# A sixteen-stage network in one kernel: an earlier search in the second attention, and joint exponentials ahead of the two state space models

## The chip, the cores and the metric

The kernel runs on one core of a Trainium2 chip. The metric is device time in microseconds (us), the time from the program's start to its end on that core. A core has five engines that run side by side, each with its own instruction stream: TensorE (PE, matrix products; its weight loads are listed as PEld), VectorE (DVE), ScalarE (ACT, functions such as exp by table), GpSimd (POOL) and SyncE (SP), which here issues DMA transfers. A stream is worked off in order, so an instruction that waits holds everything behind it on its engine. Matrix products are written to PSUM, a memory of a few banks of 128 x 512 numbers each, and the other engines read them from there.

## What is computed

A tensor x of 4 batches, 512 tokens and 128 channels (fp32) passes 16 stages of the form x = x + f(layernorm(x)): four rounds of attention a, feed-forward, attention b, feed-forward. They are called L0a L0f L0b L0f, L1a L1f L1b L1f, L2a L2f L2b L2f, L3a L3f L3b L3f. The change touches three places. The first is L0b, an attention of 16 heads of 8 dimensions that keeps the most important keys:

```python
scores = jnp.einsum('bhqd,bhkd->bhqk', q, k) * inv_sqrt_d
scores = jnp.where(causal[None, None], scores, -jnp.inf)
attn_weights = jax.nn.softmax(scores, axis=-1)
mean_importance = attn_weights.mean(axis=2)
mean_importance = mean_importance.at[:, :, -RECENCY:].set(1.0)    # RECENCY = 64
_, idx = jax.lax.top_k(mean_importance, k_keep)                    # k_keep = 391 of 512
K_keep = jnp.take_along_axis(k, idx_e, axis=2)                     # V_keep likewise
a2 = jax.nn.softmax(jnp.einsum('bhqd,bhkd->bhqk', q, K_keep) * inv_sqrt_d, axis=-1)
out = jnp.einsum('bhqk,bhkd->bhqd', a2, V_keep)
```

The other two are the state space models L2b and L3b, of which only the first steps matter here; they stand behind L2f (a mixture of 8 experts, two of which are kept for a token, beside a shared one) and L3f (a gated recurrence over the four batches):

```python
u = silu(conv(x @ in_proj_x) + conv_b)                  # 256 channels; z = x @ in_proj_z
dtr, Bc, Cc = split(u @ x_proj)                         # 64, 16, 16
delta = softplus(dtr @ dt_proj + dt_proj_b)
h = exp(delta * A) * h + (delta * u) * Bc               # scan over the 512 tokens
y = (sum_n h * Cc + u * D) * silu(z)                    # then y @ out_proj
```

## The kernel before, in words

The stages are methods of one class and run one after the other; the order of a stage's instructions is written out by hand. `keep` pins an instruction's place in the order of its engine, and `Plan` is a list of steps, each with the number of the loop step at which it is issued. Line 346 is the helper that records every matmul, so matmuls are told apart by the tile that they write.

**L0b (from line 745).** Heads are held as 4 groups g of 4 heads i; q and k have 32 rows per head, of which 8 hold the head and row 8 a one (in q) and the mask (in k); row 9 of q takes the negated largest score. Its first part is a loop over n = 0 to 67. Step n < 64 is one (batch, group, block of 128 queries): `weights(n)` does the scores of four heads (`ps_s`), adds the causal mask and finds the minimum of the negated scores in one DVE instruction per head (line 839), and takes the exponential with its sum on ACT (line 850). `invert(n - 2)` takes reciprocals (line 861), and `importance(n - 4)` adds the weighted columns up in one PSUM bank `imp` per half (two batches, 32 steps). `choose(half)` is a generator for the search: its first call copies the negated importance into `neg` (line 890) and stops; each of the next 16 does one MAX8 (line 897) and, when called again, MATCH_REPLACE8 (line 899), so 121 keys or a few more in whole eights are struck out; then it makes the mask (line 903) and issues eight DMAs on SP (line 908) that put it into row 8 of each head of k. In the loop one `next(choice)` is issued at each step with n % 7 < 4 from n = 36 on.

In the second part, unit n = 0 to 63 is one (batch, group, block of 128). `largest(n, i)` makes a head's scores of 128 queries against all 512 keys again, now with the mask, and takes the maximum on DVE (line 925). After four units `into_q` transposes these into row 9 of q: four transposes on PE and one addition on DVE (line 983). `weigh(n, i)` then makes the transposed scores `ps_st` and their exponential on ACT (line 1007), `gather` multiplies with the values, `divide`, `turn` and `project` finish. The units 0, 1, 2 of `largest` stand at n = 64, 65, 66 of the first loop. The rest is the list `stream`, in which `weigh(n)` alternates with `largest(n + 5)`; it begins with the units 3 and 4 of `largest`, and after each last head of a unit the second search (`choose(1)`) does one step. All these banks come from one ring of 7.

**L2f (line 1897).** For each batch the loop of `experts` (line 615) does 13 `hidden` steps (line 1923): two products `ps_1` and `ps_3`, ACT's Identity with bias into `t` (line 1931), DVE's product (line 1932), ACT's Silu into `hc` (line 1935); then the weighted sums `ps_o`. So m runs over 52 hidden steps, and the first steps of L2b are laid among them by the list `self.extra`: pairs of a step number m and a piece of `mamba_ahead`. Both kinds of products come from rings of four banks per tag.

**mamba_ahead (line 1973).** It prepares batch 0 of a state space model: `norm`, `turn` (transposes), `conv`, `xd`, `br`, `cr` (projections), `gate`, and the softplus, written as max(y, 0) + ln(1 + exp(-|y|)) with a correction of the rounding, for the two halves c of the 256 channels: `step(c)` (line 2069) makes `ps_dt`, DVE takes max(y, 0) into dl, ACT does Abs and Exp (2075, 2076); `log(c)` does Ln on ACT (2081) and two DVE operations (2082, 2084); `rest(c)` does three elementwise operations, on DVE for c = 0 and on POOL for c = 1 (2095), and stores dl to DRAM by a DMA on SP (2096). `spare` is true in L2f and false in L3f.

**L3f (2765 to 2791) and mamba (2143).** The end of L3f runs the pieces of `mamba_ahead` and the layer norms of batches 1 to 3 (`self.centred`, line 393: four DVE instructions of 128 x 128 each); what it leaves is in `self.late`, pairs of a scan step and a piece. The loop of `mamba` has 64 scan steps (16 per batch): a step n fetches the rates of step n + 5 from DRAM (SP, line 2268), multiplies (DVE, line 2293), scans twice (DVE, line 2298), multiplies by cr (POOL, line 2301), makes `ps_du` of step n + 1 on PE and the exponential (decay, ACT, line 2282) of step n + 3, then a piece of `prepare` for the next batch, every other step `read` (PE), and at its end the pieces of the plan.

Of the kernel before, what the change touches and what calls it, by code (L numbers as in the profile page):

```python
# [12 lines left out]
AF = mybir.ActivationFunctionType  # L13
ALU = mybir.AluOpType
# [260 lines left out]
class Net:  # L275
# [469 lines left out]
    def L0b(self):  # L745
# [7 lines left out]
        with ExitStack() as es:  # L753
# [176 lines left out]
            def split(n):  # L930
                return n // 16, n // 4 % 4, n % 4


            later = {}
            project_q(0, 0, bank("ps_qk"))
# [7 lines left out]
                    later[4 * g + h + 18] = f, 3, g  # L943
            choice = iter(())
            LATE = 4
            AHEAD = 3
            for n in range(64 + LATE):
                if n < 64:
                    weights(n)
                if n == 2:  # L950
                    rest()
                    clear(vt[0])
                if 2 <= n <= 65:
                    invert(n - 2)
                if 64 <= n < 64 + AHEAD:
                    for i in range(4):
                        largest(n - 64, i)
                if n >= LATE:
                    importance(n - LATE)
                if n == 31 + LATE:  # L960
                    choice = choose(0)
                if n in later:
                    f, b, g = later[n]
                    f(b, g, bank("ps_qk"))
                if n < 36 or n % 7 < 4:
                    next(choice, None)
            for _ in choice:
                pass
            choice = choose(1)

            def into_q(n):

                b, g, _ = split(n)
                nm = nmt[n // 4 % 2]
                pt = bank("ps_t", (P, CB, P))
                for j in range(CB):
                    self.tr(pt[:, j], nm[:, j].rearrange("p i r -> p (i r)"))  # L980
                qb = q[g][:, b * S : b * S + S]
                keep(
                    nc.vector.tensor_tensor(qb, qb, pt.rearrange("p j t -> p (j t)"), ALU.add)  # L983
                )

            def values(b):
                pv = bank("ps_v", (P, CB, 16, 8))
# [69 lines left out]
                    )  # L1057
                self.add_to_x(b, px)

            LAG = 5  # L1060
            stream = [(largest, n, i) for n in range(AHEAD, LAG) for i in range(4)]
            plan = Plan()
            for a in range(64):
                if a % 16 == 0:
# [13 lines left out]
                if a % 16 == 15:  # L1078
                    plan.at(m + 13, turn, a // 16)
                    plan.at(m + 18, project, a // 16)  # L1080

            plan.at(4 * (4 - AHEAD) + 4, into_q, 3)
            for m in range(len(stream) + 20):
                plan.run(m)
                if m < len(stream):
                    f, n, i = stream[m]
                    f(n, i)
                    if f is largest and i == 3:
                        next(choice, None)


# [805 lines left out]
    def L2f(self):  # L1897

        nc, tc = self.nc, self.tc
        NH = 13  # L1900
        with (
            tc.tile_pool(name="l2f_s", bufs=1) as sp,
            tc.tile_pool(name="l2f_r", bufs=3) as rp,
            tc.tile_pool(name="l2f_p", bufs=4, space=PSUM) as pp,
            tc.tile_pool(name="l2f_d", bufs=1, space=DRAM) as dp,
        ):
            xT, rest = self.norm(pp)
            w1, w3, w2 = self.W("f2_w1"), self.W("f2_w3"), self.W("f2_w2")
            b1, b3 = self.W("f2_b1"), self.W("f2_b3")

            def gates(b, cw):
                pl = pp.tile([P, CB, 8], F32, tag="u", name="ps_l")
                for j in range(CB):
                    c = b * S + j * P
                    self.mm(pl[:, j], xT[:, c : c + P], self.W("f2_gw"), pin=True)
                pr = self.softmax_tok(rp, pl, 8)
                bi = rp.tile([P, CB, 8], F32, name="bi")
                gb = self.row("f2_gb").unsqueeze(1).to_broadcast([P, CB, 8])
                nc.vector.tensor_tensor(bi, pr, gb, ALU.add)
                t2 = self.top2(rp, bi, pr, 8)  # L1920
                nc.vector.tensor_copy(cw, t2)

            def hidden(b, m, hc):
                n = P if m < NH - 1 else 48
                xb, cs = xT[:, b * S : b * S + S], slice(m * P, m * P + n)
                p1 = pp.tile([P, S], F32, tag="mm", name="ps_1")
                self.mm(p1[:n], w1[:, cs], xb, pin=True)
                p3 = pp.tile([P, S], F32, tag="u", name="ps_3")
                self.mm(p3[:n], w3[:, cs], xb, pin=True)
                t = rp.tile([P, S], F32, name="t")  # L1930
                nc.scalar.activation(t[:n], p1[:n], AF.Identity, bias=b1[:n, m : m + 1])  # L1931
                nc.vector.scalar_tensor_tensor(  # L1932
                    t[:n], p3[:n], b3[:n, m : m + 1], t[:n], ALU.add, ALU.mult
                )
                nc.scalar.activation(hc[:n, m], t[:n], AF.Silu)

            f = self.follow
            if f:

                def bank(name):  # L1940
                    return pp.tile([P, S], F32, tag="u", name=name)

                self.extra = tuple(
                    (at, f[n], *a, bank)
                    for at, n, *a in (
                        (4, "rates"),
                        (5, "constants"),
                        (22, "norm", 0, 1),
                        (23, "turn", 0),
                        (25, "conv", 0),  # L1950
                        (27, "conv", 1),
                        (29, "xd"),
                        (30, "step", 0),
                        (30, "step", 1),
                        (30, "log", 0),
                        (30, "log", 1),
                        (31, "rest", 0),
                        (32, "rest", 1),
                        (34, "br"),
                        (35, "cr"),  # L1960
                        (37, "gate", 0),
                        (38, "gate", 1),
                        (44, "norm", 1, 3),
                        (45, "turn", 1),
                        (46, "turn", 2),
                    )
                )
                self.late = ((0, f["norm"], 3, 4), (2, f["turn"], 3))
            self.experts(
                (sp, rp, pp, dp), NH, 48, 11, 8, 176, gates, hidden, w2, rest, bias=True  # L1970
            )

    def mamba_ahead(self, g, spare):
# [20 lines left out]
        xd = sz[:64, 0]  # L1994
        if spare:

            e0, w0, l0, e1 = (
                self.xn[:, CB * b : CB * b + CB].rearrange("p j d -> p (j d)") for b in range(B)
            )
        else:  # L2000
            m["sets"][1] = self.mamba_set(sp, 1)
            e0, w0, l0, e1 = (m["sets"][1][i][:, c] for i in range(2) for c in range(2))
        e, wl, ln = (e0, e1), (w0, sz[:, 0]), (l0, sz[:, 1])

        def rates(bank):

# [62 lines left out]
        def step(c, bank):  # L2069
# [2 lines left out]
            ps = bank("ps_dt")  # L2072
            self.mm(ps, w["dw"][:, c * P : c * P + P], xd, pin=True)
            keep(nc.vector.tensor_scalar(dl[:, c], ps, db, 0.0, ALU.add, ALU.max))
            keep(nc.scalar.activation(e[c], ps, AF.Abs, bias=db))
            keep(nc.scalar.activation(e[c], e[c], AF.Exp, scale=-1.0))

        def log(c, bank):


            keep(nc.scalar.activation(ln[c], e[c], AF.Ln, bias=ones[:, 0:1]))
            keep(nc.vector.tensor_scalar(wl[c], e[c], 1.0, None, ALU.add))
            keep(
                nc.vector.scalar_tensor_tensor(
                    wl[c], wl[c], 1.0, e[c], ALU.subtract, ALU.subtract
                )
            )

        def rest(c, bank):
            for o, x, y, op in (  # L2090
                (ln[c], ln[c], wl[c], ALU.subtract),
                (dl[:, c], dl[:, c], ln[c], ALU.add),
                (du[:, c], dl[:, c], u[:, c], ALU.mult),
            ):
                keep((nc.gpsimd if c else nc.vector).tensor_tensor(o, x, y, op))
# [14 lines left out]
            "log": log,  # L2110
            "rest": rest,
        }

# [557 lines left out]
    def L3f(self):  # L2671
# [3 lines left out]
        with (  # L2675
# [90 lines left out]
            if f:  # L2766
# [25 lines left out]


# [51 lines left out]
```

## Time and profile before

| | us |
|---|---|
| median of three runs (2464.59 to 2468.78) | 2466.05 |
| the profiled execution | 2471.9 |
| its span | 2470.2 |
| PE busy in it | 2183.7 (88%) |
| DVE busy | 1751.5 (71%) |
| ACT busy | 1307.5 (53%) |
| POOL busy | 608.9 (25%) |
| PE's weight loads, beside its products | 1025.6 (42%) |

The mean granted clock of PE is 0.926 of full speed. The span holds 32,491 instructions and 126.79 MB of DMA. In the span L0b stands at about 490 to 960, the first L2f ends and L2b begins at about 1617, and L3b runs from about 2169 to 2424.

The profile lists busy time by engine, the chain of work that ended last, and groups of instructions by line and tile. "x" before a number is a count; `out<-in` names the tiles written and read; "idle before" is the time in which the engine had nothing to run just ahead of these instructions, and the arrow names what ended it. Time is counted from the start of the span.

### The profile page before, as it was taken

The numbers are of one execution on the slowest core, as the hardware profiler recorded it, in microseconds if no ns is written. First come the engines' busy times: TensorE is split into PE (matmuls) and PEld (weight loads), VectorE is DVE, ScalarE is ACT, GpSimd is POOL, SyncE is SP. The second block draws the span as 40 slices with busy tenths as digits, with TensorE's granted clock in tenths as the row PEclk, the third lists the DMA queues.
The fourth block names the chain that finished last, engine by engine and source line by source line (L and its number), as shares of the span: only waits on it lengthen the run. The fifth ranks groups of instructions, "written<-read, shape, count | busy, mean of one in ns | idle before, by whom it ended". The sixth has DMA issues, their size and how long they took to land.

```text
span 2470.2 us, 32491 instructions
## 1 busy us (share of the span) xinstructions
PE 2183.7 (88%) x11647; PEld 1025.6 (42%) x11647; DVE 1751.5 (71%) x3544; ACT 1307.5 (53%) x2561; POOL 608.9 (25%) x431
## 2 busy tenths in 40 slices
PE   7999999999899998899877789888868998888867
PEld 2343334733233443567434345442214566422213
DVE  6666666689887675656464674579997557589995
ACT  4555554279645555342442464667635445478642
POOL 1100010010000001022152410048761015148761
PEclk9999999999799999999867889999979999989888
DMA  3000002300000000510200033235542420045540
GB/s 141 1 1 1 1 1 68 72 1 1 2 1 2 1 1 1 112 27 7 100 1 1 0 67 75 56 111 162 148 125 56 87 48 2 1 119 153 152 131 17
DMA packets 68304, 126.79 MB, mean 51 GB/s; under 512 B 9264, under 2 KB 13360, under 8 KB 67504
## 3 DMA queue, kind: packets, MB, share of 16 engines
q1 hardware_dynamic: 68144, 124.73, 19.4%
q8 instruction: 92, 1.51, 0.2%
q14 instruction: 68, 0.56, 0.1%
HBM read 118.93 MB, written 5.64 MB: 50 GB/s over the span
## 4 chain that ended last, share of the span: by engine, by line
PE 61%; DVE 26%; ACT 5%; DMA 3%; issue 2%; POOL 1%; SPq 0%; DVEq 0%; POOLq 0%; ACTq 0%
PE ps_o L346 13%; PE ps_s L346 11%; DVE hc L2298 10%; PE ps_st L346 5%; PE ps_c L346 4%; PE ps L346 4%; DVE ps_du L2293 4%; PE ps_g L346 4%; PE ps_u L346 2%; PE ps_v L346 2%; PE ps_x L346 2%; PE ps_qk L346 2%; DVE xn L393 2%; DVE e L839 2%; PE ps_q L346 2%
## 5 line engine op out<-in xcount | busy, mean ns | idle before, releaser
L2301 POOL TENSOR_TENSOR hc<-hc,cr 128x1024 f32<-128x1024 f32 x126 | 296.0, 2362 | 202.3 <-DVE hc L2298 134.7
L2298 DVE TENSOR_TENSOR_SCAN hc<-da,ps_du 128x512 f32<-128x512 f32 x256 | 298.2, 1206 | 15.6 <-ACT da L2282 2.6
L346 PE MATMUL ps_s<-k,q 32*128 32x512 f32 (+3 forms) x1088 | 275.8, 611 | 16.5 <-DVE mx L839 8.6
L346 PE MATMUL ps_du<-du,spread 64*128 64x512 f32 x512 | 167.5, 730 | 100.3 <-DVE hc L2298 97.9
L538 ACT ACTIVATE e<-ps_s,mx 128x512 f32<-128x512 f32 x256 | 172.6, 686 | 139.9 <-DVE mx L533 133.3
L2282 ACT ACTIVATE da<-da,am 128x512 f32<-128x512 f32 x244 | 165.3, 716 | 96.6 <-DMA da<-dram 82.5
L925 DVE TENSOR_REDUCE nm<-ps_s 128x1 f32<-128x512 f32 x256 | 160.4, 683 | 69.6 <-PE ps_s L346 67.8
L346 PE MATMUL ps<-xT,w_L2f 128*128 128x512 f32 (+1 forms) x416 | 197.1, 621 | 4.0 <-DVE t L1932 4.0
L1007 ACT ACTIVATE e<-ps_st 128x512 f32<-128x512 f32 x256 | 135.3, 601 | 104.9 <-PE ps_s L346 92.4
L533 DVE TENSOR_REDUCE mx<-ps_s 128x2 f32<-128x1024 f32 x128 | 150.9, 1219 | 43.8 <-PE ps_s L346 43.6
L346 PE MATMUL ps_st<-q,k 32*128 32x512 f32 x512 | 167.3, 632 | 6.5 <-DVE q L983 5.5
L2293 DVE TENSOR_TENSOR ps_du<-ps_du,br 128x1024 f32<-128x1024 f32 x128 | 154.8, 1210 | 12.4 <-PE ps_du L346 12.4
L850 ACT ACTIVATE e<-e,mx 128x512 f32<-128x512 f32 (+3 forms) x256 | 140.2, 549 | 20.6 <-DVE mx L839 20.0
L346 PEld LDWEIGHTS ps_s<-k,q 32*128 32x128 f32 x1088 | 96.5, 198 | 113.1 <-DVE mx L839 52.7
L346 PEld LDWEIGHTS ps_du<-du,spread 64*128 64x128 f32 x512 | 46.0, 209 | 214.2 <-DVE hc L2298 184.5
L346 PE MATMUL ps_s<-q,k 64*128 64x512 f32 x512 | 129.1, 618 | 2.2 <-ACT e L538 1.7
L346 PE MATMUL ps_c<-e,vz 128*64 128x512 f32 x512 | 123.5, 604 | 0.8 <-POOL vz L549 0.8
L1932 DVE SCALAR_TENSOR_TENSOR t<-ps,w_L2f,t 128x512 f32<-128x512 f32 (+1 forms) x104 | 76.8, 746 | 63.5 <-PE ps L346 44.4
L346 PEld LDWEIGHTS ps<-xT,w_L2f 128*128 128x128 f32 (+1 forms) x416 | 76.6, 193 | 101.4 <-issue 75.2
L839 DVE CUSTOM_DVE_ANT_0 e<-ps_s,tri 128x512 f32<-128x512 f32 (+3 forms) x256 | 109.6, 484 | 10.1 <-PE ps_s L346 10.1
L1931 ACT ACTIVATE t<-ps,w_L2f 128x512 f32<-128x512 f32 (+1 forms) x104 | 69.7, 682 | 87.3 <-PE ps L346 84.4
L549 POOL TENSOR_TENSOR vz<-v,z 128x512 f32<-128x512 f32 x32 | 33.4, 1043 | 322.0 <-DVE z L547 293.0
(505 smaller groups left out, 4235.1 us busy)
## 6 DMA issues: line engine op xcount, KB each, us to landing
da<-dram SPq DMA_DIRECT2D x244, 256.0 KB
wt<-dram SPq DMA_DIRECT2D x144, 128.0 KB
wt<-dram SPq DMA_DIRECT2D x32, 256.0 KB
dram<-dl SPq DMA_DIRECT2D x16, 256.0 KB
wt<-dram SPq DMA_DIRECT2D x16, 224.0 KB
wt<-dram SPq DMA_DIRECT2D x16, 192.0 KB
wt<-dram SPq DMA_DIRECT2D x16, 160.0 KB
w_L2f<-w_L2f SPq DMA_DIRECT2D x1, 2433.0 KB
```

The source lines that it names most:

```text
L346: i = self.nc.tensor.matmul(out, lhsT, rhs, start=start, stop=stop)
L533: nc.vector.tensor_reduce(mx, sc, AX.X, ALU.max, negate=True)
L538: nc.scalar.activation(es[n][:, hh], sc[:, hh], AF.Exp, bias=mx[:, hh : hh + 1], accum_out=z[m][:, j, hh : hh + 1],)
L839: red = nc.vector.tensor_tensor_reduce(e[:, i, :w], sc[i][:, :w], tri[:, S - w :], -1.0, BIG, ALU.add, ALU.min, mx[:, i : i + 1],)
L850: nc.scalar.activation(e[:, i, :w], e[:, i, :w], AF.Exp, bias=mx[:, i : i + 1], scale=-1.0, accum_out=z[:, i : i + 1],)
L925: nc.vector.tensor_reduce(nm[:, j, i, 9:10], sc, AX.X, ALU.max, negate=True)
L1007: keep(nc.scalar.activation(es_[n][:, i], sc, AF.Exp))
L1932: nc.vector.scalar_tensor_tensor(t[:n], p3[:n], b3[:n, m : m + 1], t[:n], ALU.add, ALU.mult)
L2282: keep(nc.scalar.activation(da[n][:, t], src, AF.Exp, scale=am[:, at : at + 1]))
L2293: nc.vector.tensor_tensor(dx[n], dx[n], sets[b % 2][4].unsqueeze(1).to_broadcast([P, 2, S]), ALU.mult)
L2298: nc.vector.tensor_tensor_scan(hc[n][:, t], da[n][:, t], dx[n][:, t], 0.0, ALU.mult, ALU.add)
L2301: (nc.vector if n == 16 * B - 1 else nc.gpsimd).tensor_tensor(hc[n], hc[n], sets[b % 2][5].unsqueeze(1).to_broadcast([P, 2, S]), ALU.mult)
```

## The change

In L0b five units of `largest`, 0 to 4, stand at n = 62 to 66 of the first loop (three units at 64 to 66 before); at n = 66 `into_q(3)` stands behind the first head's maximum. The search does a step at n % 3 < 2 in place of n % 7 < 4. The copy into `neg` of the second search stands right behind the first loop; its 16 steps begin at entry 16 of `stream`, which starts empty.

In L2f the two halves' exponentials become one of 128 x 1024 (`exps`), the two logarithms and what follows them likewise (`logs`); behind each, `self.prime(AF.Silu)` has ACT do a small Silu. The pieces stand at other hidden steps, and the two gates behind `rest`.

In L3f `centred(2)` and `centred(3)` stand ahead of L3b, behind `step(0)` and `cr`; `log(1)` and `rest(1)` stand at scan step 1, the third turn and the gates one step later than before. The addition of 1 for the half c = 1 is done by ACT.

```diff
@@ L0b, first loop
-            AHEAD = 3
+            LAG = 5
             for n in range(64 + LATE):
...
-                if 64 <= n < 64 + AHEAD:
-                    for i in range(4):
-                        largest(n - 64, i)
+                if 62 <= n < 62 + LAG:
+                    largest(n - 62, 0)
+                    if n == 66:
+                        into_q(3)
+                    for i in range(1, 4):
+                        largest(n - 62, i)
                 if n >= LATE:
                     importance(n - LATE)
...
-                if n < 36 or n % 7 < 4:
+                if n < 36 or n % 3 < 2:
                     next(choice, None)
             for _ in choice:
                 pass
             choice = choose(1)
+            next(choice)
@@ L0b, stream
-            LAG = 5
-            stream = [(largest, n, i) for n in range(AHEAD, LAG) for i in range(4)]
+            stream = []
...
-            plan.at(4 * (4 - AHEAD) + 4, into_q, 3)
...
-                    if f is largest and i == 3:
+                    if f is largest and i == 3 and m >= 16:
                         next(choice, None)
@@ L2f, self.extra
                         (30, "step", 0),
-                        (30, "step", 1),
-                        (30, "log", 0),
-                        (30, "log", 1),
-                        (31, "rest", 0),
-                        (32, "rest", 1),
-                        (34, "br"),
-                        (35, "cr"),
-                        (37, "gate", 0),
-                        (38, "gate", 1),
+                        (31, "step", 1),
+                        (32, "br"),
+                        (33, "exps"),
+                        (34, "cr"),
+                        (36, "logs"),
+                        (37, "rest", 0),
+                        (38, "rest", 1),
+                        (40, "gate", 0),
+                        (41, "gate", 1),
@@ mamba_ahead
-            keep(nc.scalar.activation(e[c], ps, AF.Abs, bias=db))
-            keep(nc.scalar.activation(e[c], e[c], AF.Exp, scale=-1.0))
+            keep(nc.scalar.activation(half(e, c), ps, AF.Abs, bias=db))
+            if not spare:
+                keep(nc.scalar.activation(e[c], e[c], AF.Exp, scale=-1.0))
-        def log(c, bank):
-            keep(nc.scalar.activation(ln[c], e[c], AF.Ln, bias=ones[:, 0:1]))
-            keep(nc.vector.tensor_scalar(wl[c], e[c], 1.0, None, ALU.add))
...
+        def exps(bank):
+            keep(nc.scalar.activation(e, e, AF.Exp, scale=-1.0))
+            self.prime(AF.Silu)
+
+        def log(e, wl, ln, by_act=False):
+            if by_act:
+                keep(nc.scalar.activation(wl, e, AF.Identity, bias=ones[:, 0:1]))
+            else:
+                keep(nc.vector.tensor_scalar(wl, e, 1.0, None, ALU.add))
+            keep(nc.scalar.activation(ln, e, AF.Ln, bias=ones[:, 0:1]))
+            keep(nc.vector.scalar_tensor_tensor(wl, wl, 1.0, e, ALU.subtract, ALU.subtract))
+
+        def logs(bank):
+            log(e, wl, ln)
+            self.prime(AF.Silu)
...
+            "log": lambda c, bank: log(e[c], wl[c], ln[c], by_act=c == 1),
@@ L3f
                 f["step"](0, bank)
+                self.centred(2, keep)
                 f["log"](0, bank)
...
                 f["cr"](bank)
+                self.centred(3, keep)
                 f["turn"](1, bank)
                 self.late = (
-                    (0, lambda bank: self.centred(2, keep)),
                     (0, f["step"], 1),
-                    (0, f["log"], 1),
-                    (0, f["rest"], 1),
-                    (1, lambda bank: self.centred(3, keep)),
+                    (1, f["log"], 1),
+                    (1, f["rest"], 1),
                     (2, f["turn"], 2),
-                    (3, f["turn"], 3),
-                    (4, f["gate"], 0),
-                    (5, f["gate"], 1),
+                    (4, f["turn"], 3),
+                    (5, f["gate"], 0),
+                    (6, f["gate"], 1),
                 )
```

More of the change, by code (lines that the diff above doesn't have):

```diff
@@ L931, in split, with into_q @@
                 return n // 16, n // 4 % 4, n % 4
+            def into_q(n):
+                b, g, _ = split(n)
+                nm = nmt[n // 4 % 2]
+                pt = bank("ps_t", (P, CB, P))
+                for j in range(CB):
+                    self.tr(pt[:, j], nm[:, j].rearrange("p i r -> p (i r)"))
+                qb = q[g][:, b * S : b * S + S]
+                keep(
+                    nc.vector.tensor_tensor(qb, qb, pt.rearrange("p j t -> p (j t)"), ALU.add)
+                )
             later = {}
@@ L969, in L0b @@
             choice = choose(1)
[L974 to L984, printed above, removed]
+            next(choice)
             def values(b):
@@ L1995, in mamba_ahead @@
         if spare:
-            e0, w0, l0, e1 = (
-                self.xn[:, CB * b : CB * b + CB].rearrange("p j d -> p (j d)") for b in range(B)
+            e, ln = (
+                self.xn[:, n : n + 8].rearrange("p (c j) d -> p c (j d)", c=2) for n in (0, 8)
             )
+            wl = sz
         else:
@@ L2002, in mamba_ahead @@
             e0, w0, l0, e1 = (m["sets"][1][i][:, c] for i in range(2) for c in range(2))
-        e, wl, ln = (e0, e1), (w0, sz[:, 0]), (l0, sz[:, 1])
+            e, wl, ln = (e0, e1), (w0, sz[:, 0]), (l0, sz[:, 1])
         def rates(bank):
@@ L2074, in step, with half @@
             keep(nc.vector.tensor_scalar(dl[:, c], ps, db, 0.0, ALU.add, ALU.max))
-            keep(nc.scalar.activation(e[c], ps, AF.Abs, bias=db))
-            keep(nc.scalar.activation(e[c], e[c], AF.Exp, scale=-1.0))
-        def log(c, bank):
-            keep(nc.scalar.activation(ln[c], e[c], AF.Ln, bias=ones[:, 0:1]))
[L2082 to L2087, printed above, removed]
+            keep(nc.scalar.activation(half(e, c), ps, AF.Abs, bias=db))
+            if not spare:
+                keep(nc.scalar.activation(e[c], e[c], AF.Exp, scale=-1.0))
+        def half(t, c):
+            return t[:, c] if spare else t[c]
+        def exps(bank):
[11 more added lines that the diff above has]
+            self.prime(AF.Silu)
         def rest(c, bank):
+            l, v = half(ln, c), half(wl, c)
             for o, x, y, op in (
-                (ln[c], ln[c], wl[c], ALU.subtract),
-                (dl[:, c], dl[:, c], ln[c], ALU.add),
+                (l, l, v, ALU.subtract),
+                (dl[:, c], dl[:, c], l, ALU.add),
                 (du[:, c], dl[:, c], u[:, c], ALU.mult),
@@ L2109, in mamba_ahead @@
             "step": step,
-            "log": log,
+            "exps": exps,
+            "logs": logs,
+            "log": lambda c, bank: log(e[c], wl[c], ln[c], by_act=c == 1),
             "rest": rest,
```

## The prediction

> **What bounds the kernel now.** I read the page first (PE busy 88% of the span, DVE 71%, ACT 53%; the chain that ended last is PE 61%, DVE 26%), which says only that the bound changes by stage. So I read three places: the end of the second attention's weighing (L0b), the block before the first state space model (L2f), and the start of the second (L3b). In each I took the chain of waits, then the timeline by engine, then the windows.
>
> L0b, chain of waits (start, length, what):
> ```profile
> 667.17 1.71 DMA k<-mask
> 669.02 2.09 PE ps_s L346 x8
> 671.11 1.84 PE imp L346 x8
> 672.95 1.11 PE ps_s L346 x8
> 674.06 7.30 DVE nm L925 x12
> 682.40 1.87 DVE nm L925 x3
> 684.27 0.55 DVE m L897
> 684.85 0.70 DVE neg L899 x2
> 685.54 0.60 DVE q L983
> 686.19 1.22 PE ps_st L346
> ```
> The search's last step has just made the mask. Its DMA holds the first `largest`, DVE stands idle from 667.06 to 671.10, and then works through 20 maxima, the copy `neg`, one search step and the addition into q before the stream starts at 686.19. From 694 to 760 PE is busy 65.08 of 66.00 us, from 760 to 940 179.49 of 180.00: there PE is the bound.
>
> L2f, windows (length, then PE, PEld, DVE, ACT, POOL busy, then granted clock, DMA share and GB/s):
> ```profile
> 1556.00:1560.00 4.00, 0.57 (x2) 0.17 (x2) 3.79 (x4) 3.97 (x7) 2.94 (x3) 1.00 0.00 0
> 1560.00:1563.00 3.00, 2.48 (x5) 0.86 (x4) 2.30 (x4) 2.53 (x5) 2.71 (x2) 0.54 0.51 180
> 1563.00:1566.00 3.00, 3.00 (x5) 1.32 (x4) 0.00 (x0) 1.28 (x2) 0.00 (x0) 0.50 0.36 127
> ```
> and PE's timeline (start, length, what, in brackets the idle time ahead and what ended it):
> ```profile
> 1559.43 1.16 PE L346 MATMUL ps<-xT,w_L2f 128*48 128x512 f32 x2 [3.96 <-DVE t L1932]
> ```
> PE waits 3.96 us for a bank and then runs at half clock.
>
> L3b, DVE's timeline:
> ```profile
> 2144.09 1.11 DVE L393 TENSOR_SCALAR xn<-x,ln_mv,ln_rs 128x128 f32<-128x128 f32 x4
> ...
> 2173.18 3.19 DVE L393 TENSOR_SCALAR xn<-x,ln_mv,ln_rs 128x128 f32<-128x128 f32 x4
> ...
> 2180.55 0.41 DVE L2082 TENSOR_SCALAR sz<-sz 128x512 f32<-128x512 f32 x1
> 2180.89 2.37 DVE L393 TENSOR_SCALAR xn<-x,ln_mv,ln_rs 128x128 f32<-128x128 f32 x1
> ```
> The same four normalisations take 1.11 us alone and 3.19 beside POOL's product, in the path of the scans, where DVE is the bound (2230 to 2400: 164.3 of 170 us).
>
> **The change part by part.** Sums are made against the profiled execution, 2471.9 us (span 2470.2), 5.9 above the median 2466.05; I take the same difference off both.
>
> *Search sooner (L0b).* The 16 steps stay, each MAX8 and MATCH_REPLACE8, 1.25 us of the chain; they now stand in two of three weighing steps, not four of seven, and in DVE's new order the last step and the mask stand before weighing step 59 instead of after 63. Eight mask DMAs (4.43 us of issue on SP, the first landed after 1.71) move with them; nothing else is queued on SP there, and PE's scores of steps 60 and 61 don't wait for them. The first `largest` follows step 62, some 7 us after the issue at 2.7 us a step (72.8 us for 27), so DVE's idle 4.0 us go. The denser steps cost nothing in sum, as DVE does the same work; but DVE idled 6.6 of 75.5 us there, 6.0 for PE's scores at a granted clock of 0.77. Evening out may win most of this (4) or, if PE stays at half clock, lose 2. I take 0.
>
> *Largest scores earlier, `into_q(3)`, `neg`.* Units 0 to 4 issue the same 20 matmuls and 20 maxima (0.61 each). On PE unit 0 goes ahead of `imp` 58 and the scores of step 63; those wait with it if the mask is late. What leaves the path ahead of the first weigh: three maxima behind the addition (1.87), the copy `neg` (0.6), one search step (1.25). They run on DVE beside the stream, where DVE has 8.6 us free in 694 to 760. With the DMA wait: 4.0 + 1.87 + 0.6 + 1.25 = 7.7 us. The second search starts two units later and ends three later, at unit 18; its mask is read at unit 27, so that costs nothing. If PE is at half clock in steps 62 to 66, its 8.9 us of matmuls there (from the same forms at full clock) become up to 17.8, against 14 on DVE: lower end 7.7 − 4 = 3.7.
>
> *Joint exponentials before L2b (L2f).* From 1533.9 to the first `ps_o` at 1568.6 PE has 25.2 us of work: ten hidden steps at 1.72, two `ps_dt` 1.9, `br` and `cr` 3.9, a turn 0.44, two `ps_z` 1.74. The other 9.5 are waits (0.64 + 0.56 + 3.96 + 0.52 = 5.7) and half clock (3.8). ACT caused them: seven table loads of 1.28, five of them in the 12 us before 1560. Now there are six, and the softplus is two blocks: load, exp of 1024 (1.06, row of L2231), load, prime (0.20) = 3.8 us; and load, Ln (1.15), load, prime = 3.9 us. I walked the new order with these rows. The first block runs about 1546.7 to 1550.6; `t` of step 35 then reaches DVE by 1551.85, which frees the bank PE wants at 1550.9: a wait of 0.95. The second runs 1554.0 to 1558.0; steps 37 and 38 leave ACT by 1560.9, PE needs them in `ps_o` at 1560.6: 0.3. `ps_o` so starts at 1533.9 + 25.2 − 1.74 (gates now after it) + 0.95 = 1558.3. Gain 10.3 − 1.74 − 0.3 = 8.3 us. Queues: the two `dl` stores now hold the later `wt` fetches on SP until POOL's `rest` ends about 1559.4; the weigh that needs them stands at about 1561, and DVE's next operand comes from PE at 1566, so up to 4 us are hidden; beyond that each is paid. Gates still come ahead of the first gated step, 50 us later.
>
> Here a rule speaks against the row. The Trainium skill, page "ScalarE: Activation LUTs", section "What ACT_TABLE_LOAD costs", puts a switch of sets at the load's 1.28 us plus a drain of about 1.38. In the trace the load at 1550.25 lasts 1.28 and its activation starts at 1551.54: no drain. By the page each block would be 2.8 longer, PE's wait 3.7 and half clock would follow (3.8 more): gain 8.3 − 2.8 − 3.8 = 1.7. I take the row, and keep 1.7 as the lower end; the upper is 9.5.
>
> *Seam before L3b (L3f).* `centred(2)` and `centred(3)` leave DVE's path beside POOL: by the chain 3.10, and 0.24 + 2.30 + 1.49, and the addition of the logarithm 0.33, in sum 7.46. They go into DVE's idle 1.42 us before 2163.10 (it waits for ACT's exp) and 1.37 before 2169.31 (it waits for `ps_du`); 1.1 each without POOL, so hidden by 0.3; without that cover, 2.2. The addition goes to ACT as Identity, 0.69. The same page, section "Rules for kernel authors", wants additions on VectorE. By the row that is 0.41 there against 0.69 on ACT; if ACT were the bound the change would lose 0.7, but DVE waited here for nobody and ACT was idle 1.69 at 2176.5. I take the gain. `log` and `rest` stand one scan step later: Ln ends about 2181.8, two POOL operations of 1.27 end 2184.4, then the `dl` store, now issued at 2186.64; the fetch of scan 8 behind it lands by about 2193, needed at 2201. The next late thing is ACT's softplus of the next batch, which in the new order stands before the decay of scan 11 (about 2215, now read at 2224.87): gain at most 9.7. PE's slow stretch (granted 0.57 in 2190 to 2196) may stay; I take 7.5, lower end 3.
>
> Sum: 7.7 + 8.3 + 7.5 = 23.5 us; 2471.9 becomes 2448.4, the median 2442.5.
>
> **The rivals.**
> *Half of it is taken by the next engine.* PE at half clock in the last weighing steps (3.7 left), longer blocks on ACT (5), ACT behind DVE in L3b (3): 12 us, 2454. For it: granted clock 0.77 in the search, ACT busy 29.71 of 30 us in 2200 to 2230. Against: PE stops waiting in L2f.
> *More goes than is counted.* DVE's idle 6.6 us in the search shrink by 4, L3b gains 9.7: 29.7, 2436. For it: PE's 5.99 us wait at 2189.91, then slow matmuls, depended on the normalisations. Against: the clock of 0.77.
> *The stream's clock falls, and it is slower.* Weighing (686 to 950, 264 us) is bound by PE at clock 1.00[...]. DVE now starts it with `neg` and three maxima in arrears, so PE can wait for banks in the first units. It decides from a mean clock of 0.90: 264 × (1/0.90 − 1) = 29 us. At 0.89 it is 33, so 2476. Against: PE busy 65.08 of 66 us beside 15 search steps.
> *The mask did not hold it.* If another wait takes the 4 us and both seams only shift theirs (1.7 and 0): within 5 us, 2463.
>
> **How the numbers follow.** The forecast 0.51, the first rival 0.19, the second 0.17, slower 0.08, no change 0.05. The range runs from the second rival's 2436, less 2 for a smaller wait in L2f, to the first's 2454, plus 3 if L2f then gives its lower end (1.7 in place of 5): 2434 to 2457. About 0.2% (5 us) is what a measurement here can tell from no change: faster 0.87, within 0.05, slower 0.08.
>
> **What would show it.** L0b: the first `ps_st` within 9 to 12 us of weighing step 63's last score plus the maxima, no DMA in the chain, 7 to 8 us less from 591 to 686. L2f: PE's longest wait before `ps_o` below 1.5 us, granted clock 1.00 through it, two loads in each softplus block. L3b: L393 at 1.1 us for four, scan 4 ending about 2188 minus the earlier shifts instead of 2195.7. The prediction is wrong if PE's granted clock over 686 to 950 is below 0.95, if `ps_o` in L2f still waits over 3 us, or if the decay of scan 8 or 11 ends last in L3b by more than the 7 us won.

## The result, and the profile after

The changed kernel takes 2446.94 us (median of four runs, 2443.98 to 2450.05), the kernel before beside it 2467.41: a ratio of 0.991 (0.9894 to 0.9925), so 22 us less, 18.5 to 26 by the interval (the two medians differ by 20.5). A second measurement (e12_after_again) gave 0.9904 (0.9888 to 0.9919). The profiled execution took 2443.98 us, with a span of 2442.1 against 2470.2 and a mean granted clock of 0.929 against 0.926. One execution of e7_centred, the one that was profiled, ran at a granted clock of 0.55 and took 3528.25 us; it is left out, and e7b_centred_again stands for its profile.

**The page.** The engines do nearly the same work (PE 2183.7 to 2178.1 us, DVE 1751.5 to 1746.9, ACT 1307.5 to 1306.3). What went is waiting.

```profile
span 2442.1 us, 32490 instructions
PE 2178.1 (89%) x11647; PEld 1027.6 (42%) x11647; DVE 1746.9 (72%) x3541; ACT 1306.3 (53%) x2561; POOL 609.4 (25%) x431
```

**L0b**, chain of waits of the changed kernel (start, length, what). The mask is made at 652.03 and its DMA is not in the chain; four units of maxima stand among the last weighing steps, and the last three maxima run beside PE's `imp` and `ps_v`, as the sum had it. The first `ps_st` comes into the chain at 675.72 (it starts at 675.64) in place of 686.19.

```profile
652.03 0.39 DVE mask L903
...
668.47 2.38 DVE nm L925 x4
...
670.89 0.33 PE ps_t L351
671.22 1.11 PE ps_s L346 x6
672.33 1.44 PE imp L346 x16
673.76 1.95 PE ps_v L346 x8
675.72 0.62 PE ps_st L346
```

**L2f**, PE's timeline and then DVE's (the brackets hold the idle time ahead and what ended it). The wait of 3.96 us in a hidden step is gone and `ps_o` starts at 1542.63. But 24 products later PE waits 4.02 us for the last `hc`, and the 28 products behind this wait take 4.92 us, where they take 3.36 in e10 at a granted clock of 1.00.

```profile
1535.43 7.36 PE L346 MATMUL ps<-xT,w_L2f 128*128 128x512 f32 x16
1542.63 2.84 PE L346 MATMUL ps_o<-w_L2f,hc 128*128 128x128 f32 x24
1549.49 4.92 PE L346 MATMUL ps_o<-w_L2f,hc 73*128 73x128 f32 x28 [4.02 <-ACT hc L1936]
```

```profile
1543.81 1.76 DVE L2109 TENSOR_TENSOR xn<-xn,sz 128x512 f32<-128x512 f32 x1
1545.61 1.63 DVE L2109 TENSOR_TENSOR dl<-dl,xn 128x512 f32<-128x512 f32 x1
1547.28 0.69 DVE L2109 TENSOR_TENSOR du<-dl,u 128x512 f32<-128x512 f32 x1
1547.88 2.06 DVE L1933 SCALAR_TENSOR_TENSOR t<-ps,w_L2f,t 48x512 f32<-48x512 f32 x3
```

L2109 is `rest`. Its first two operations last over twice as long as the third, while POOL runs the other half (1542.07 to 1546.7), and the products `t` of the last hidden steps stand behind them.

**L3b**, DVE's timeline. Four normalisations now take 1.11 us in both places, but the second multiplication waits 2.18 us for PE, which it did not before.

```profile
2143.89 1.11 DVE L393 TENSOR_SCALAR xn<-x,ln_mv,ln_rs 128x128 f32<-128x128 f32 x4
...
2150.14 1.11 DVE L393 TENSOR_SCALAR xn<-x,ln_mv,ln_rs 128x128 f32<-128x128 f32 x4
...
2157.73 1.23 DVE L2309 TENSOR_TENSOR ps_du<-ps_du,br 128x1024 f32<-128x1024 f32 x1 [2.18 <-PE ps_du L346]
```

The windows of the seam, before and then after (length, then PE, PEld, DVE, ACT, POOL busy, granted clock, DMA share and GB/s). Before, PE stood nearly still for 6 us and then worked off its arrears at a clock of 0.57; after, at the same time behind the start of the scans, it runs at 1.00 throughout.

```profile
2184.00:2190.00 6.00, 0.09 (x2) 0.09 (x2) 6.00 (x7) 3.72 (x7) 3.87 (x4) 0.86 0.12 45
2190.00:2196.00 6.00, 6.00 (x14) 2.33 (x16) 5.60 (x5) 0.04 (x1) 4.80 (x3) 0.57 0.65 175
```

```profile
2166.00:2172.00 6.00, 4.98 (x14) 1.77 (x15) 5.93 (x7) 5.02 (x9) 5.92 (x5) 1.00 0.24 82
2172.00:2178.00 6.00, 6.00 (x25) 2.12 (x23) 5.79 (x6) 4.84 (x7) 5.20 (x3) 1.00 0.87 226
```

### The profile page after: what moved, and what is told of

Same layout as the page of the kernel before. It is cut to its first block, busy times and chain, and to the rows that moved or that the text cites. A ratio compares the mean times of both kernels' runs of the same rounds, so it can differ in the third digit from the quotient of the medians.

```text
span 2442.1 us, 32490 instructions
## 1 busy us (share of the span) xinstructions
PE 2178.1 (89%) x11647; PEld 1027.6 (42%) x11647; DVE 1746.9 (72%) x3541; ACT 1306.3 (53%) x2561; POOL 609.4 (25%) x431
## 4 chain that ended last, share of the span: by engine, by line
PE 61%; DVE 26%; ACT 5%; issue 3%; DMA 2%; POOL 2%; SPq 1%; DVEq 0%; POOLq 0%; ACTq 0%
PE ps_o L346 13%; PE ps_s L346 11%; DVE hc L2314 9%; PE ps_st L346 5%; PE ps_c L346 5%; PE ps L346 4%; DVE ps_du L2309 4%; PE ps_g L346 4%; PE ps_u L346 2%; PE ps_v L346 2%; PE ps_x L346 2%; PE ps_qk L346 2%; DVE e L839 2%; PE ps_q L346 1%; PE ps_tr L351 1%
## 5 line engine op out<-in xcount | busy, mean ns | idle before, releaser
L346 PE MATMUL ps_s<-k,q 32*128 32x512 f32 (+3 forms) x1088 | 278.1, 601 | 10.3 <-DVE mx L839 7.4
L659 DVE TENSOR_TENSOR hc<-hc,wt 128x1024 f32<-128x1024 f32 x80 | 94.6, 1188 | 23.3 <-ACT hc L1936 12.3
```

What stands on the lines that cost most here:

```text
L346: i = self.nc.tensor.matmul(out, lhsT, rhs, start=start, stop=stop)
L659: nc.vector.tensor_tensor(h, h, wt[b, k][:, r:e], ALU.mult)
```

## The experiments

**How a stretch is measured.** All kernels have the same 11,647 matmuls, in the same order but for the changed spots. So I take the start of the k-th matmul in two traces, one ahead of a place and one behind it, and compare the times between. The table lists what each stretch takes beside the first profile of the kernel before, in us. L0b runs from scores at 522.86 into the stream (714.33), L2f from 1498.89 to a `ps_dl` of L2b at 1618.19, L3b from `ps_dl` at 2169.05 to scan 20 (2256.36; scans are counted from 0).

| | kernels with this stage unchanged | with all edits of it | partly |
|---|---|---|---|
| L0b | 0, -1.40, -0.23, -0.19, -0.24 | -10.87, -13.20, -11.93, -11.62, -13.29 | e5 -5.48, e9 -4.46, e6 -10.46 |
| L2f | 0, 0.13, -1.42, -2.14, -4.12, -1.99, -3.04, -2.14 | -4.67, -2.44, -3.36 | e10 -5.66, e4 -7.91 |
| L3b | 0, -0.02, 1.32, 1.33, 1.87, 0.0 | -9.41, -9.42, -9.43, -9.42, -9.41 | e7b -2.52, e8 -0.33 |

The means of the first two columns differ by 11.8, 1.65 and 10.2 us, in sum 23.6. The first column is worth a look: the same instructions in L2f spread over 4.3 us, so the 1.65 is little more than the scatter of its means. Taken from the first `ps_dt`, where the change of L2f begins, the eight kernels need 81.86 to 84.45 us to the same end (mean 83.10), the three with all edits 81.02 to 82.43 (81.59): again 1.5 less.

**e1_l0b, e2_l2f, e3_l3b: the three places alone.**

```diff
  e1: kernel before + the hunks of L0b
  e2: kernel before + the hunks of L2f and mamba_ahead (no addition on ACT)
  e3: kernel before + the hunk of L3f, and in log, for c = 1 in L3f alone:
+             keep(nc.scalar.activation(wl[c], e[c], AF.Identity, bias=ones[:, 0:1]))
```

> The kernel before with the edits to the second attention (L0b) alone. By the two traces the matmuls behind the search stand 10.9 us earlier in the changed kernel than ahead of it. If the three places are worth what their own stretch shows and add up: 10.9 us less, ratio about 0.9956. Prediction's sum for this part: 7.7 us (0.9969). Rival, that a part of the 10.9 is chance of the granted clock (0.82 to 0.71 in the search before, 0.87 to 0.74 after): about 6 us, and PE's matmul at the first ps_o stands 6 us, not 10.9, earlier.

> The kernel before with the joint exponentials and logarithms and their new places in L2f alone. By the two traces the first ps_o comes 10.6 us earlier, but 7.4 of this is given back (4.0 in one wait of PE for the last hc). If that holds: 3.2 us less, ratio 0.9987. The prediction's term was 8.3 us (0.9966). Rival: the wait of 4.0 us is only there because of what came earlier in the changed kernel, then about 7 us.

> The kernel before with the edits at the seam between L3f and L3b alone (two normalisations moved ahead of the scans, the logarithm and what follows it a scan step later, one addition on ACT). By the two traces: 10.8 us earlier at scan 9, 9.4 us after the fetches of the next batch. If that holds: 9.4 us less, ratio 0.9962. Prediction's term: 7.5 us (0.9970). Rival, that PE's half clock before (0.57) was chance and returns: 5 us or less.

Measured: 0.9953 (0.9938 to 0.9968), 0.9989 (0.9981 to 0.9997) and 0.9955 (0.9941 to 0.9969); of the 2471.5 us beside them 11.6, 2.7 and 11.1. All three agree with their stretches, and the rivals (6 us; 7 us; 5 us or less) fall. The product of the ratios is 0.9897, the changed kernel stood at 0.991 and 0.9904: the parts add up within the intervals.

**e5_rate, e9_units_only: the search's rate against the units' place.**

```diff
  e5: kernel before
-                if n < 36 or n % 7 < 4:
+                if n < 36 or n % 3 < 2:
  e9: e1_l0b
-                if n < 36 or n % 3 < 2:
+                if n < 36 or n % 7 < 4:
```

> The kernel before with the search at two of three weighing steps alone; the units of largest scores stay at n = 64 to 66. The search's edits together took 10.9 us from the stretch between the search and the first ps_o. Theory: the wait for the mask's DMA (4.0 us) goes, and DVE's idle time for PE's scores in the search shrinks by about 3 (6.0 before, 2.7 after): 7 us less in that stretch, the other 4 belong to the units' place. Rival A (the prediction's sum): only 4.0 us. Rival B: the wait for the DMA is replaced by a later one, since units still stand behind it: under 2 us.

> All edits of the second attention, but the search at the old rate of four in seven steps, so that the mask is written behind the first two units' scores. Those two units take their largest scores of the first heads before the mask is in k, that is over all 512 keys, an upper bound of the largest kept score. Theory: the units hide the mask's DMA as well as the earlier search does, so 4 (DMA) and 4 (maxima, neg, a search step off the path) come from the units; only the 3 us of DVE's idle time in the search come from the rate: 8 us less in the stretch to the first ps_o. Rival: without the earlier search the later units' scores wait for the DMA as before: about 4 us.

Measured: 0.9977 (0.9969 to 0.9985) and 0.9989 (0.9979 to 1.0). In the stretch they gain 5.1 and 4.1 against the unchanged mean of -0.41, together 9.2 of the 11.8. So e5 lies between its theory (7) and rival A (4.0), and in e9 the rival holds. Most of e9's gain, 2.65 us, stands between the first `ps_st` and the first `ps_o`: 5.52 us there, as in all kernels with the units moved and the second search later, against 8.17 in the mean of those without an edit of L0b and 8.54 in e5. The chain of e9 shows why it wins so little ahead of that: the mask's DMA holds the scores of the later units as before.

```profile
670.28 0.40 DVE mask L903
670.73 0.12 POOL neg L886
670.87 1.72 DMA k<-mask
672.58 0.14 issue
672.72 2.09 PE ps_s L346 x8
```

The chain of e5 has no DMA, but 20 maxima in a row, `neg`, a search step and the addition stand ahead of the first `ps_st`; PE waits 4.5 us there for that addition.

```profile
664.88 2.37 DVE nm L925 x4
667.34 7.20 DVE nm L925 x12
674.53 0.53 DVE neg L890
675.13 0.46 issue
675.58 1.88 DVE nm L925 x3
677.46 0.55 DVE m L897
678.03 0.70 DVE neg L899 x2
678.73 0.60 DVE q L983
679.38 1.22 PE ps_st L346
```

**e6_second_search: the second search where it was.**

```diff
  e1_l0b
-            next(choice)
-                    if f is largest and i == 3 and m >= 16:
+                    if f is largest and i == 3:
```

> The edits of the second attention alone, but the second search as before: its copy neg is issued inside the stream and its steps from the stream's first unit on. Prediction's term: the copy and a search step off the path, 1.85 us; then the stretch to the first ps_o gains 10 us or less in place of the 11.9 that the edits of this stage show. Rival: the stream's entry is bound by PE (13.84 of 14 us in the changed kernel), so DVE's order there is worth nothing: 11.9 within 0.5.

Measured: 0.9962 (0.9947 to 0.9977), stretch -10.46; with all edits the mean is -12.18 and the smallest gain 10.87. By that alone the 1.85 could be real. But DVE's timeline shows a wait of 2.60 us for PE just ahead of the four maxima before `neg`, so `neg` (0.61) and the step have room.

```profile
674.59 1.89 DVE L925 TENSOR_REDUCE nm<-ps_s 128x1 f32<-128x512 f32 x3 [0.33 <-PE ps_s L346]
679.07 2.48 DVE L925 TENSOR_REDUCE nm<-ps_s 128x1 f32<-128x512 f32 x4 [2.60 <-PE ps_s L346]
681.47 0.61 DVE L890 TENSOR_SCALAR neg<-imp 128x448 f32<-128x448 f32 x1
```

The first `ps_st` parts the two. Up to it, where e6 leaves the order as in e1, e6 takes 155.08 us of the stretch, and the five kernels with all edits 152.65 to 155.07. From it to the end of the stretch, where its edit acts, e6 takes 25.94 us and all five 25.53 or 25.54. So the place of the second search is worth 0.4 us, and the rival holds; the other 1.3 lie where nothing was edited. `neg` starts in e6 behind the first `ps_st` (681.47 against 677.87): it is the units' earlier place that takes the copy and the search step off the path to it.

**e4_rest_later, e10_split: L2f's new wait, and the join.**

```diff
  e4: changed kernel
-                        (37, "rest", 0),
-                        (38, "rest", 1),
-                        (40, "gate", 0),
-                        (41, "gate", 1),
+                        (40, "rest", 0),
+                        (41, "rest", 1),
+                        (42, "gate", 0),
+                        (43, "gate", 1),
  e10: changed kernel
-                        (33, "exps"),
...
-            if not spare:
-                keep(nc.scalar.activation(e[c], e[c], AF.Exp, scale=-1.0))
+            keep(nc.scalar.activation(half(e, c), half(e, c), AF.Exp, scale=-1.0))
```

> The changed kernel with the three elementwise operations of each half behind the logarithms (rest) at hidden steps 40 and 41 in place of 37 and 38, and the two gates at 42 and 43. Theory: in the changed kernel these stand on DVE ahead of the last hidden step's product, run at 1.76, 1.63 and 0.69 us beside POOL, and so hold the last hc and PE by 4.0 us. Moved behind it, that wait goes: 4 us less than the changed kernel (about 2443 where it takes 2447), ratio to the kernel before 0.9895. Rival: the last hc waits for ACT, whose logarithm block (3.9 us) stands there anyway: the wait stays, no change, 0.991.

> The changed kernel with the exponentials of L2f not joined: each half's Exp right behind its Abs at hidden steps 30 and 31, the logarithms joined as they are. Two loads more and 6.4 in place of 3.8 us of ACT. Theory, that the join is what counts: PE's waits before the first ps_o return, 2 to 4 us slower than the changed kernel in the stretch of L2f. Rival, that the places count and ACT has room at steps 30 to 32 (it waits 2.5 and 0.5 us for PE there): the same within 0.5 us.

Measured, e4: 0.9894 (0.9877 to 0.991). In the trace the wait falls from 4.02 to 0.88 us and the three operations run at 0.68, 0.69 and 0.69. The stretch is 4.4 us shorter than the mean of the three changed kernels. The theory holds for the wait; by time alone e4 (0.9894) can't be told from the changed kernel (0.991, 0.9904).

```profile
1548.40 2.84 PE L346 MATMUL ps_o<-w_L2f,hc 128*128 128x128 f32 x24
1552.12 3.36 PE L346 MATMUL ps_o<-w_L2f,hc 73*128 73x128 f32 x28 [0.88 <-ACT hc L1936]
```

Measured, e10: 0.9891 (0.9874 to 0.9908), stretch -5.66. Without the join L2f is no slower, if anything 2.2 us quicker, so the theory falls for the stretch, and the rival's "the same within 0.5" is not met either. From the first `ps_dt` to the first `ps_o` the theory is nearly right: 25.72 us, against 23.77 in all three traces with the join, since PE waits 1.73 us ahead of the transposes. It is won back behind that: PE waits 2.54 us for the last `hc`, not 4.02, and the 28 products after it take 3.36 us, against 4.92, 6.23 and 5.94 in the three, at a granted clock of 0.71, 0.50 and 0.50 from 31 to 36 us behind the first `ps_dt`.

```profile
1537.59 0.66 PE L351 MATMUL ps_tr<-ident,cw 128*128 128x128 f32 x4 [1.73 <-DVE t L1933]
...
1550.65 3.36 PE L346 MATMUL ps_o<-w_L2f,hc 73*128 73x128 f32 x28 [2.54 <-ACT hc L1936]
```

So of the 9.5 us by which the first `ps_o` came forward (33.30 in the mean of the eight kernels, 23.77), the joint exponentials brought 2.0. The other 7.6 belong to the pieces' places and the joint logarithms, which e10 keeps; no run parts these two. e4 and e10 together were not tried either.

**e7_centred, e7b_centred_again, e8_log_later: the seam in two halves.**

```diff
  e7, e7b: kernel before
                 f["step"](0, bank)
+                self.centred(2, keep)
...
                 f["cr"](bank)
+                self.centred(3, keep)
...
-                    (0, lambda bank: self.centred(2, keep)),
...
-                    (1, lambda bank: self.centred(3, keep)),
  e8: e3_l3b
                 self.late = (
+                    (0, lambda bank: self.centred(2, keep)),
...
+                    (1, lambda bank: self.centred(3, keep)),
  (and without the two lines ahead of it)
```

> The kernel before with the two normalisations of batches 2 and 3 (centred) moved ahead of L3b, the rest of the seam as before. The seam's edits together took 10.8 us at scan 9 and 9.4 behind the fetches. Theory: the normalisations are the most of it: by the chain of before 3.10 + 0.24 + 2.30 + 1.49 = 7.1 us, and PE's 6.0 us wait at scan 4 shrinks with them: 7 to 9 us less. Rival: the chain only passes to ACT, whose logarithm of step 0 (two loads) then ends last: 3 us or less.

> The kernel before with the second half's logarithm, its addition on ACT, and what follows it a scan step later (turn and gates too), and the normalisations where they were. Theory: DVE's path keeps its 7.1 us of normalisations, only the addition (0.33) and its wait leave: 0 to 2 us less. Rival, that the order of the logarithm is what counts and the normalisations fill a wait that is there anyway: 5 us or more less.

> The kernel with the two normalisations (centred) moved alone, once more for its profile. Its time was 5.9 us less (ratio 0.9976). Theory: within the seam, from the last of L3f to scan 11, its matmuls come 7 to 9 us earlier; L393 lasts 1.1 us for four in each place and PE's wait at scan 4 (6.0 us before) falls below 2. Rival: 3 us or less, because the logarithm of step 0 on ACT, with two loads, then holds the decays of scans 3 and 4.

Measured: e7 0.9976 (0.9966 to 0.9987), e7b 0.9989 (0.9976 to 1.0001), e8 0.9978 (0.997 to 0.9987). In the stretch e7b gains 2.5 and e8 0.3 us where both together gain 9.4. So the rival holds for e7b by size, though not by its reason: the chain of waits has no ACT at scans 3 and 4. By time e7 gave 5.9 us and e7b 2.7, and the interval of e7b reaches from nothing to that. e8 is as its theory had it. In e7b DVE's timeline shows two things that keep the time: the addition, still on DVE and still in scan step 0, takes 1.68 us, after which PE waits 2.1 us for scan 2; and the multiplication of scan 9 waits 4.61 us for PE, whose granted clock was 0.60 from 2207 to 2215.

```profile
2178.34 1.23 DVE L2293 TENSOR_TENSOR ps_du<-ps_du,br 128x1024 f32<-128x1024 f32 x1 [3.65 <-PE ps_du L346]
...
2183.49 1.68 DVE L2082 TENSOR_SCALAR sz<-sz 128x512 f32<-128x512 f32 x1
...
2215.03 1.23 DVE L2293 TENSOR_TENSOR ps_du<-ps_du,br 128x1024 f32<-128x1024 f32 x1 [4.61 <-PE ps_du L346]
```

The second is the larger: at scan 8 e7b is 4.2 us ahead of the kernel before, at scan 9 2.7. The same multiplication waits 3.2 us in the other kernels without the later logarithm, turn and gates, and 0.45 in e8 and in all five with both edits.

In e8 the second set of normalisations takes even 4.26 us beside POOL, and PE then waits 4.87 us for scan 2. At scan 4 e8 is 2.7 us behind the kernel before; at scan 9 it is 1.8 ahead.

```profile
2182.76 4.26 DVE L393 TENSOR_SCALAR xn<-x,ln_mv,ln_rs 128x128 f32<-128x128 f32 x4
```

The whole-kernel gain of e8, 5.4 us, is more than its seam shows. In the trace its L2f, which it does not touch, is 3.0 us ahead of the first profile of before; the rest is not explained.

**e12_after_again.**

> The changed kernel once more, for the sum of the parts: L0b 11.6, L2f 2.7, L3b 11.1 (times of the parts alone) make 25.4 us less if they add up, ratio 0.9897; the first measurement gave 0.991 (0.9894 to 0.9925). Rival: the parts overlap and it stays at 0.991 or above, 22 us or less. The version with rest later stood at 0.9894; if its 4 us are real, this one is at about 0.991.

Measured: 0.9904 (0.9888 to 0.9919), or 23.7 us of 2472.6, between theory and rival; the interval covers both.

## Why the prediction was right, and where its terms were not

The forecast was 23.5 us. The three stretches sum to 23.6 and the times to 22 and 24, so direction and sum held. But the terms did not: L0b and L3b gave more than their terms and L2f much less, and that the sum still came to 23.5 is luck. Of the three signs that the prediction named for being wrong, one came: `ps_o` in L2f waited over 3 us.

*L0b: 7.7 predicted, 11.8 measured.* The DMA's 4.0 us went as forecast. Two terms were missing. One is the "I take 0" for DVE's idle time in the search: DVE waited 6.0 us for PE's scores between 591 and 686, and 2.7 from 589 to 676 in the changed kernel; over all traces the means are 5.5 without an edit of L0b and 2.8 with all of them. The other is the entry of the stream: from the first `ps_st` to the first `ps_o` 8.1 us before (686.19 to 694.32), 5.5 after (675.64 to 681.17). By difference this leaves some 2.4 us for the 3.7 of maxima, copy and step; no run shows them singly. The lower end (PE at half clock) appeared in part, a granted clock of 0.85 from 652 to 676, and was paid out of the gain; in e4 and e12 the same piece ran at 1.00.

*L2f: 8.3 predicted, 1.65 measured (2.7 by time).* Here the working failed. Up to the first `ps_o` the walk was good: 10.3 predicted, 10.9 seen against the first profile (34.63 to 23.77 us from the first `ps_dt`). The step "steps 37 and 38 leave ACT by 1560.9, PE needs them in `ps_o` at 1560.6: 0.3" failed. It followed ACT's block and left out `rest` on DVE, which stands ahead of the product for step 38 and is slowed by its own other half on POOL; the wait was 4.02, so 3.7 more. The 28 products behind that wait took 1.6 to 2.9 us more than at full clock, 2.3 in the mean of three traces, and the sum had nothing for it. So 8.3 + 0.5 - 3.7 - 2.3 = 2.8, which is what the three traces show against the first profile (84.36 to 81.59). e4 moves `rest`, and both the wait and the slow products go. The last failure is the profile that the sum was made against: to the first `ps_o` it took 34.63 us, the eight kernels with this stage unchanged 32.62 to 34.69, so up to 2 us of its half clock (3.8) were chance; to the end it is 1.3 above their mean.

That the gain came out at the 1.7 that the rule of a drain gave as lower end is luck: in the changed kernel the load lasts 1.28 and the Exp starts right behind it, again without a drain.

```profile
1532.36 1.28 ACT L2085 ACT_TABLE_LOAD   x1
1533.65 1.06 ACT L2085 ACTIVATE xn<-xn 128x1024 f32<-128x1024 f32 x1
```

And "ACT caused them" holds in part: two loads more (e10) put the first `ps_o` 2.0 us back, but the stretch was not longer for it.

*L3b: 7.5 predicted, 9.4 to 10.2 measured.* The mechanism was the forecast's (the normalisations leave DVE's path beside POOL), the size near that of the second rival (9.7). Of the 7.46 us of DVE 2.18 came back at once as a wait for PE's `ps_du`, which the sum had left out. In return PE's 6 us standstill and its slow arrears went: at the multiplication of scan 4 the gain was 4.9 us (2192.03 to 2169.42, less the 17.7 that the kernel was ahead), at scan 9 10.8 (2216.33 to 2187.78). The sum had nothing for the wait at scan 9 either (3.18 us before, 0.45 after), which the later logarithm and gates took away. About 1.4 were given back behind it (the stretch to scan 20 shows 9.4), where the decays wait for the next batch's rates: POOL's softplus product, the `dl` store and fetches of 5.94 us are the chain there. e7b and e8 show that the gain needs both edits; the prediction had credited almost all of it to the first.

*The rivals.* The stream kept a granted clock of 1.00 from 690 to 926, so the slower case did not come. The first rival's "next engine" came in L2f, but it was DVE, not ACT with longer blocks; the second rival's mechanism came in L0b and L3b.

## What to carry to other kernels

When a step is moved onto an engine's queue, list every instruction of that step by engine, and ask of each which product stands behind it; in L2f the block on ACT was watched and three elementwise operations on DVE cost the gain. A stretch in which one engine waits and then works at half clock can hold more than the chain shows, and two edits there can be worth more together than apart: 2.5 and 0.3 us alone, 9.4 joined, as each left the other's wait standing. Before a few microseconds of half clock are booked as a gain, look at how much the same stretch varies in other executions.

## What was not expected of the hardware

The same instructions of L2f and the start of L2b took from 119.42 us (e1, mean granted clock 0.94) to 115.18 us (e6, 0.97) in eight executions of kernels that leave this stage as it was; on the whole, the longer the stretch, the lower the clock, and no wait of theirs was edited. Nor does a wait alone settle the clock: in the kernel before PE waited 3.96 us ahead of 1559.43 and then ran at 0.54, but it waited 1.80 us ahead of 2180.45 and ran at 1.00 from 2178 to 2184. The Trainium skill, page "TensorE: Matmul & The Clock Gate", section "What's actually happening", says that the activity window runs free, so that the slow start of a kernel varies from run to run. It puts the cost of that start below 1% of a typical span; here the spread of one stretch in the middle of the kernel is 0.17% of the span, about a fifth of the change's whole gain. That the free window is the cause here is not shown.

DVE slows beside POOL by more than twice with two inputs (1.76 and 1.63 against 0.69 us for 128x512) and with one (4.26 against 1.11 us for four of 128x128, 1.68 against 0.43 for 128x512). In L2f the two slow ones each end 0.55 us behind the POOL operation that ran beside them (1545.57 behind 1545.02, 1547.24 behind 1546.69), as if they had stood until it was done; no run tests that. The Trainium skill, page "GPSIMD Engine Reference", section "Specifications", names such contention for DVE instructions with two inputs in SBUF and for those in a 2-port mode; whether the ones with one input ran in that mode no trace here shows.
